# Third sequence's projections ahead of the first feed-forward block, two inputs sent through memory, one weight kept for three products, and ScalarE's pieces placed behind single products

## The chip, the cores and the metric

The kernel runs on one core of one Trainium2 chip. The metric is device time in microseconds. The kernel before took 823.38 us, the median of three runs (822.4 to 823.66).

## What is computed

The input x has 4 sequences of 512 tokens by 512 features, in float32. Each sequence goes through a gated scan and then through a feed-forward block (FFN) with a Walsh-Hadamard transform (fwht) of its 2048 hidden features. Cut to what matters, with `norm` for a layer norm without weights:

```python
def attn(h):                                  # h = norm(x)
    i, f, g = h @ Wi.T, h @ Wf.T, h @ Wg.T    # 512 x 512 each
    gate = sigmoid(f)
    v = silu(i) * (1 - gate)
    o = scan over t of  o[t] = gate[t] * o[t-1] + v[t]
    o = o * rsqrt(mean(o * o) + 1e-5) * gnorm_w * g * sigmoid(g)
    return o @ Wo.T

def ffn(h):                                   # h = norm(x)
    hidden = silu(h @ W1.T) * (h @ W3.T)      # 512 -> 2048
    return fwht(hidden) @ W2.T                # 2048 -> 512

x = x + norm(attn(norm(x)))
x = x + norm(ffn(norm(x)))
```

## The kernel before

**Products.** Every 512x512x512 product is done as seven half-size products of quarter blocks instead of eight (a Strassen-Winograd scheme). `combine_left` and `combine_right` make the sums of blocks S1 to S4 and T1 to T4 with four VectorE operations each. `seven` lists the seven products P1, P2, P6, P5, P7, P3, P4 in this order. Each is eight 128x256 matmuls into one of three PSUM banks X, Y, Z: X serves P1, P6, P7 and P4, Z serves P5 and P3, Y serves P2. P6 adds onto what P1 left in X, so it may start only when ScalarE's copy behind P1 (L418) has read the bank; P3 likewise waits for the copy behind P5, and P4 for VectorE's add behind P7 (L416).

**Units.** A sequence's attention has three units of seven products: (b,0) and (b,1) make i and f for half the features each, (b,2) makes g. At the end of (b,0) and (b,1) `gates` runs on ScalarE and VectorE, ending in the scan; at the end of (b,2) `output_gate` makes `og`, and squares o for the mean square. The out-projection `attn_out(b)` has seven products and one step `squares`, a sum over partitions by 1-column matmuls; its end, `done`, adds the residual (`OutputNorm.half`, whose ScalarE part is L316) and normalizes the result as input 'f' of the FFN (`normalize_tiles`; the scale is applied by ScalarE at L266, after `nb` from VectorE, L233). An FFN has eight units `ffn_unit(b, m)` of seven products and four groups `ffn_out(b, part)` of seven.

**Order.** TensorE's and SP's orders are those of the program text; the other engines' orders are made by a scheduler from priorities (`tc.high_priority`) and from `behind(what)`, which keeps an instruction from going ahead of the latest one of that name on its engine. `run` issues a unit's seven products. After a product it runs what `beside` holds for that place, and, in all places of a dense unit or in places 1, 3, 5 and 6 of another, takes one step from the queue `fill`. In this way out-projections and second FFN products are laid between the products of a unit. Before the change the order is: attention of sequences 0 and 1, FFN 0, attention 2, FFN 1, attention 3, FFN 2, FFN 3; `attn_out(1)` lies in FFN 0, `attn_out(2)` in FFN 1, `attn_out(3)` in FFN 2.

**Transposed inputs.** A normalized input must be turned before it multiplies. For those in `ON_TENSOR` TensorE does it in two steps of eight 128x128 transposes (L348), with copies from PSUM by VectorE and ScalarE (L355, L353). The others go through memory: ScalarE writes the tile in a permuted order, POOL's queue stores it (L275, `xnd`), SP's queue loads it as a `fold` (L371), and VectorE transposes it in 32x32 blocks (L383).

**Weights and buffers.** Weights come through SP's queue in tiles of 896 KB, five buffers in `stream` and four in `stream2`. The first time, a weight is loaded raw (L164), combined, and stored with its sums by POOL's queue (L145); later it is loaded whole (L152). `wo` is loaded for each out-projection by `again`. The matrix W2 is transformed on the way: `transform_high` on TensorE (L646), `butterfly_a` and `butterfly_b` on VectorE with stores by POOL (L665), then `load_low`, `low_pair` and `low_tile` during FFN 0. The pieces of W2 (`w2p`) lie in the buffers `ht` (four) and `stream2`.

Of the kernel before, what the change touches and what calls it, by code (L numbers as in the profile page):

```python
# [14 lines left out]
P = 128  # L15
# [29 lines left out]
def kernel(  # L45
# [56 lines left out]
    beside = {}  # L102

    def run(products, dense):
        for k, make in enumerate(products):
            make()
            for other in beside.pop(k, ()):
                other()
            if dense or k in (1, 3, 5, 6):
                slot()  # L110
# [127 lines left out]
    ON_TENSOR = ("a", 0), ("a", 1), ("f", 0)  # L238
# [124 lines left out]
    def load_fold(b, name):  # L363


        folds[name, b] = t = work.tile(
            [P, T // 32, P], F32, tag="wide", name=f"fold_{name}_{b}", bufs=3
        )
        rows = xnd[name, b].rearrange("t p d -> (t p) d")
        for i in range(4):  # L370
            nc.sync.dma_start(  # L371
                out=t[ts(i, 32)],
                in_=rows[:, ts(i, P)].rearrange("(g q) k -> q g k", q=32),
            )

    def transpose_fold(b, name):


        fold = folds.pop((name, b)).rearrange("p (h g) k -> p h g k", h=2)
        xt = work.tile([P, 7, 2, H], F32, tag="xt", name=f"xt_{name}_{b}", bufs=2)  # L380
        for c in range(ND):
            to = xt[:, B11 : B12 + 1 : B12 - B11] if c < 2 else xt[:, B21 : B22 + 1]
            nc.vector.transpose(  # L383
                to[:, :, c % 2, :].rearrange("p h (g q) -> p h g q", q=32),
                fold[:, :, :, ts(c, 32)],
            )
# [68 lines left out]
    def attn_unit(b, u, dense=False):  # L455
# [14 lines left out]
        def output_gate(d):  # L470
# [7 lines left out]
            nc.scalar.activation(o, o, AF.Square)  # L478
            nc.vector.tensor_add(o[:, 0], o[:, 0], o[:, 1])
            nc.vector.tensor_add(o[:, 0, 0], o[:, 0, 0], o[:, 0, 1])  # L480
# [19 lines left out]
    def attn_out(b):  # L500
# [8 lines left out]
        w = wo_t.pop(b) if b in wo_t else [again(("wo", c), b, stream2) for c in range(2)]  # L509
# [13 lines left out]
        def done(i, j):  # L523
            with tc.high_priority(offset=SOON):
# [3 lines left out]
                if j == 1 - i:  # L528
                    y[1].half(i)
                    normalize_tiles(b, "f", 2 * i, 2)  # L530
# [243 lines left out]
    attn_unit(0, 2)  # L774
    load_attn_w(1, 1)
    fill.extend([None] * 3 + attn_out(0))
    attn_unit(1, 0, True)
    with behind("P7"):
        butterfly_b(2)
        butterfly_a(3)  # L780
        butterfly_b(3)
    load_attn_w(1, 2)
    attn_unit(1, 1, True)
    load_ffn_w(0, 0)
    load_low(0)
    fill.extend([None] + transposes(0, "f"))
    attn_unit(1, 2)
# [3 lines left out]
    LOW = {1: (0, "combined", 0), 3: (1, "P2", 2), 5: (2, "P2", 2), 6: (3, "P2", 2)}  # L791
    for b in range(B):
        last = b == B - 1
        for m in range(NU):
# [13 lines left out]
            if m == 0 and not last:  # L808
                fill.extend([None] * (4 if b else 2) + attn_out(b + 1))
# [6 lines left out]
            if m == 2 and b == 0:  # L816
                load_x(2)
            if m == 4 and b + 2 < B:
                with behind("P7"):
                    late = [normalize_tiles(b + 2, "a", i, 2, True) for i in (0, 2)]  # L820
            if m in (4, 5) and b + 2 < B:
                for t, k in enumerate((3, 5) if m == 4 else (0, 3)):
                    beside.setdefault(k, []).append(
                        partial(behind_copy, partial(late[m - 4], range(t, t + 1)))
                    )
            if m == 6 and not last:
                load_fold(*((b + 2, "a") if b + 2 < B else (b + 1, "f")))
            if m == NU - 1 and not last:
                transpose_fold(*((b + 2, "a") if b + 2 < B else (b + 1, "f")))
# [4 lines left out]
        if b + 2 < B:  # L834
            load_attn_w(b + 2, 0)
            load_fold(b + 1, "f")
            fill.extend([None] + tail)
            for u in range(3):
                if u < 2:
                    load_attn_w(b + 2, u + 1)  # L840
# [47 lines left out]
```

## Time and profile before

| | us |
|---|---|
| median of three runs | 823.38 |
| the profiled execution | 822.66 |
| its span, first to last instruction | 820.9 |
| TensorE matmuls busy | 801.8 (98%) |
| VectorE busy | 492.3 (60%) |
| ScalarE busy | 262.3 (32%) |
| GpSimd busy | 66.3 (8%) |

The span is the time between the first and the last instruction; the profiled execution's own time is 1.8 us more. A busy share says how long an engine had something in work; as matmul records overlap and their ends are modelled, the starts of the records say more about TensorE. The profile's timeline gives instructions in order of time, with an idle time ahead of one and what ended it in brackets. The view of waits adds up such idle times by engine and cause. In names like `X_a<-xt_a,wi` the output stands ahead of the arrow, with the buffer numbers left out; `_a` is attention, `_f` the FFN, `_y` an out-projection and `_po` the second FFN product.

### The profile page before, as it was taken

To read this page: it belongs to the slowest core of one execution; us is meant where nothing else is said; L and a number is where in the kernel's file an instruction comes from. 1 tells how busy PE (TensorE), PEld (TensorE's weight loads), DVE (VectorE), ACT (ScalarE), POOL (GpSimd) and SP (SyncE) were. 2 spreads that over 40 slices of the span, in tenths; PEclk is the share of its full clock that TensorE was granted. 3 is DMA by queue.
4 is the path that set the end of the run, shared out by engine and by line. 5 is a ranking of instruction groups with operands and counts; after the bars stand their busy time and mean duration, and the time that the engine had idled before them with its cause. 6 is when DMAs were issued, how large, how long until landed. Compare 5 with 4: busy or idle time off the path is not lost.

```text
span 820.9 us, 9770 instructions
## 1 busy us (share of the span) xinstructions
PE 801.8 (98%) x3696; PEld 695.9 (85%) x3696; DVE 492.3 (60%) x982; ACT 262.3 (32%) x372; POOL 66.3 (8%) x103
## 2 busy tenths in 40 slices
PE   6999999999999999999999999999999999999995
PEld 4788887888888888888888888888888888888884
DVE  5899789697797457355345646536345334534345
ACT  4553453253321334235312233326211111322111
POOL 2120100122110001011000000102000000100000
PEclk9999999999999999999999999999999999999998
DMA  9985468778998217744538433726463542625201
GB/s 328 406 310 199 142 174 291 260 265 305 332 265 334 91 46 285 310 152 170 229 97 242 161 143 123 288 90 214 156 216 117 208 179 91 235 111 199 80 11 52
DMA packets 64207, 162.19 MB, mean 198 GB/s; under 512 B 4384, under 2 KB 37792, under 8 KB 64160
## 3 DMA queue, kind: packets, MB, share of 16 engines
q1 hardware_dynamic: 55248, 118.31, 41.8%
q0 software_dynamic: 8192, 41.95, 12.9%
q10 hardware_dynamic: 720, 1.31, 0.4%
q8 instruction: 29, 0.48, 0.2%
q14 instruction: 18, 0.15, 0.0%
HBM read 118.56 MB, written 42.99 MB: 197 GB/s over the span
## 4 chain that ended last, share of the span: by engine, by line
PE 88%; DVE 5%; DMA 4%; ACT 1%; issue 1%; SPq 1%; POOL 0%; POOLq 0%; DVEq 0%
PE X_f L431 25%; PE X_po L564 13%; PE Z_f L431 12%; PE X_a L431 8%; PE Z_po L564 7%; PE Y_f L431 6%; PE Z_a L431 4%; PE Y_po L564 3%; PE X_y L517 3%; DMA wo<-s_wo 3%; PE Y_a L431 2%; PE h L646 2%; PE Z_y L517 2%; PE Y_y L517 1%; DVE x L321 1%
## 5 line engine op out<-in xcount | busy, mean ns | idle before, releaser
L431 PE MATMUL X_f<-xt_f,w 128*128 128x256 f32 x1024 | 241.9, 379 | 0.3 <-ACT d_f L418 0.3
L431 PEld LDWEIGHTS X_f<-xt_f,w 128*128 128x128 f32 x1024 | 194.0, 190 | 27.1 <-ACT d_f L418 0.7
L418 ACT COPY d_f<-X_f 128x512 f32<-128x512 f32 x96 | 56.0, 584 | 290.9 <-PE X_f L431 266.6
L431 PE MATMUL Z_f<-xt_f,w 128*128 128x256 f32 x512 | 121.1, 379 | 1.1 <-ACT d_f L418 1.1
L564 PE MATMUL X_po<-w,ht 128*128 128x256 f32 x512 | 120.9, 379 | 0.2 <-DVE f L416 0.2
L431 PEld LDWEIGHTS Z_f<-xt_f,w 128*128 128x128 f32 x512 | 97.2, 190 | 14.7 <-ACT d_f L418 1.5
L564 PEld LDWEIGHTS X_po<-w,ht 128*128 128x128 f32 x512 | 97.2, 190 | 13.7 <-DVE f L416 0.6
L416 DVE TENSOR_TENSOR f<-X_po,f 128x512 f32<-128x512 f32 x51 | 35.1, 687 | 93.8 <-PE X_po L564 87.6
L446 DVE TENSOR_TENSOR ht<-d_f 128x1024 f32<-128x1024 f32 x32 | 39.0, 1219 | 62.6 <-ACT d_f L540 48.9
L564 PE MATMUL Z_po<-w,ht 128*128 128x256 f32 x256 | 60.5, 379 | 0.0
L431 PE MATMUL Y_f<-xt_f,w 128*128 128x256 f32 x256 | 60.5, 379 | 0.0
L564 PEld LDWEIGHTS Z_po<-w,ht 128*128 128x128 f32 x256 | 48.6, 190 | 6.6
L431 PEld LDWEIGHTS Y_f<-xt_f,w 128*128 128x128 f32 x256 | 48.6, 190 | 6.6
L418 ACT COPY d_a<-X_a 128x512 f32<-128x512 f32 x36 | 21.0, 583 | 89.9 <-PE X_a L431 81.7
L225 POOL TENSOR_TENSOR rs_f<-rs_f,power 128x2 f32<-128x2 f32 x16 | 14.2, 891 | 416.4 <-DVE nm_f L313 395.9
L416 DVE TENSOR_TENSOR d_f<-X_f,d_f 128x512 f32<-128x512 f32 x32 | 22.1, 690 | 27.7 <-PE X_f L431 27.7
L416 DVE TENSOR_TENSOR d_f<-Z_f,d_f 128x512 f32<-128x512 f32 x32 | 22.1, 690 | 22.1 <-PE Z_f L431 22.1
L540 ACT ACTIVATE d_f<-d_f 128x1024 f32<-128x1024 f32 x32 | 33.8, 1055 | 0.9
L431 PE MATMUL X_a<-xt_a,wi 128*128 128x256 f32 x128 | 33.2, 382 | 0.8 <-ACT w2p L647 0.7
L431 PE MATMUL X_a<-xt_a,wf 128*128 128x256 f32 x128 | 32.8, 379 | 0.0
L517 PE MATMUL X_y<-wo,og 128*128 128x256 f32 x128 | 30.7, 380 | 0.9 <-DMA wo<-s_wo 0.8
L416 DVE TENSOR_TENSOR f<-Z_po,f 128x512 f32<-128x512 f32 x28 | 19.2, 686 | 20.5 <-PE Z_po L564 20.5
(163 smaller groups left out, 1007.3 us busy)
## 6 DMA issues: line engine op xcount, KB each, us to landing
w<-s_w SPq DMA_DIRECT2D x72, 896.0 KB, 6.4
s_w<-w POOLq DMA_DIRECT2D x24, 896.0 KB, 6.9
w<-in_W_dram SPq DMA_DIRECT2D x32, 256.0 KB, 5.6
wi<-s_wi SPq DMA_DIRECT2D x6, 896.0 KB, 10.6
wf<-s_wf SPq DMA_DIRECT2D x6, 896.0 KB, 6.7
wg<-s_wg SPq DMA_DIRECT2D x6, 896.0 KB, 5.8
wo<-s_wo SPq DMA_DIRECT2D x6, 896.0 KB, 9.3
w_h<-w2p POOLq DMA_DIRECT2D x8, 512.0 KB, 5.9
```

Of the source, the lines that this page charges most:

```text
L225: read["power"] = nc.gpsimd.tensor_tensor(r, r, power_t[:, 0:n], ALU.pow)
L321: nc.vector.scalar_tensor_tensor(x_t, self.y[:, i, t, :], r[:, t : t + 1], x_t, ALU.mult, ALU.add)
L416: read[what] = nc.vector.tensor_add(to, ps[which], to)
L418: read["copy"] = nc.scalar.copy(to, ps[which])
L431: nc.tensor.matmul(ps[:, n, :], w[:, a, c, :], xt[:, bb, c, :], start=first and n == 0 and c == 0, stop=c == 1, skip_group_check=True,)
L446: nc.vector.tensor_mul(to.rearrange("p (t k) f -> p k t f", t=2), a.rearrange("p k (t f) -> p k t f", t=2), b2.rearrange("p k (t f) -> p k ...
L517: nc.tensor.matmul(ps[:, t, :], og[:, a, c, ts(t, P)], w[c][:, bb, :], start=first and t == 0 and c == 0, stop=c == 1, skip_group_check=True,)
L540: nc.scalar.activation(d[:, 0], d[:, 0], AF.Silu)
L564: nc.tensor.matmul(ps[:, t, :], hts[b, m][:, a, ts(t, P)], w[m][:, W2[bb], :], start=first and t == 0 and m == ms[0], stop=m == ms[-1], sk ...
L646: nc.tensor.matmul(p, h_sb, t[:, k, :], start=True, stop=True)
```

## The change

It makes six edits.

1. `acts` is a new queue of ScalarE pieces. `run` takes one of them after each product and places it behind the latest copy. The scaling of input 'f' (four pieces per sequence) and the Square of `output_gate`, now in two halves, go there.
2. The first FFN's input leaves `ON_TENSOR` and goes through memory.
3. The three attention units of sequence 2 stand ahead of FFN 0, with `attn_out(1)` between their products; `attn_out(2)` lies in FFN 0, and `attn_out(3)` in FFN 2 as before. The normalized input of sequence 2 is made beside unit (1,1), stored, loaded as a fold after it, and transposed beside unit (1,2). The fold of FFN 0's input is loaded after unit (2,0) and transposed beside the last products of (2,1).
4. A fold is now two tiles of 128 KB DMAs, eight loads instead of four, and eight VectorE transposes of 128x256 instead of four of 128x512; a fold may lie in two `ht` buffers.
5. The weight `wo` that is loaded for sequence 0 stays in its two buffers for sequences 1 and 2; only sequence 3 loads it again.
6. The butterflies `butterfly_b(2)`, `butterfly_a(3)` and `butterfly_b(3)` move from behind unit (1,0) to unit (2,0); x of sequences 2 and 3 is loaded at other places.

```diff
@@ -100,10 +100,14 @@
                 make()
 
     beside = {}
+    acts = deque()
 
     def run(products, dense):
         for k, make in enumerate(products):
             make()
+            if acts:
+                with behind("copy"):
+                    acts.popleft()()
             for other in beside.pop(k, ()):
                 other()
             if dense or k in (1, 3, 5, 6):
@@ -235,7 +239,7 @@
 
     xns, xnd = {}, {}
 
-    ON_TENSOR = ("a", 0), ("a", 1), ("f", 0)
+    ON_TENSOR = ("a", 0), ("a", 1)
 
     def normalize_tiles(b, name, i0, n, later=False):
 
@@ -360,30 +364,39 @@
 
     folds = {}
 
-    def load_fold(b, name):
-        folds[name, b] = t = work.tile(
-            [P, T // 32, P], F32, tag="wide", name=f"fold_{name}_{b}", bufs=3
-        )
+    def load_fold(b, name, tag="wide"):
+        G = T // 64
+        if tag == "ht":
+            t = [
+                work.tile([P, G, P], F32, tag=tag, name=f"fold_{name}_{b}_{h}", bufs=4)
+                for h in range(2)
+            ]
+        else:
+            both = work.tile([P, 2, G, P], F32, tag=tag, name=f"fold_{name}_{b}", bufs=3)
+            t = [both[:, h] for h in range(2)]
+        folds[name, b] = t
         rows = xnd[name, b].rearrange("t p d -> (t p) d")
-        for i in range(4):
-            nc.sync.dma_start(
-                out=t[ts(i, 32)],
-                in_=rows[:, ts(i, P)].rearrange("(g q) k -> q g k", q=32),
-            )
+        for h in range(2):
+            for i in range(4):
+                nc.sync.dma_start(
+                    out=t[h][ts(i, 32)],
+                    in_=rows[ts(h, H), ts(i, P)].rearrange("(g q) k -> q g k", q=32),
+                )
 
     def transpose_fold(b, name):
 
 
-        fold = folds.pop((name, b)).rearrange("p (h g) k -> p h g k", h=2)
+        fold = folds.pop((name, b))
         xt = work.tile([P, 7, 2, H], F32, tag="xt", name=f"xt_{name}_{b}", bufs=2)
-        for c in range(ND):
-            to = xt[:, B11 : B12 + 1 : B12 - B11] if c < 2 else xt[:, B21 : B22 + 1]
-            nc.vector.transpose(
-                to[:, :, c % 2, :].rearrange("p h (g q) -> p h g q", q=32),
-                fold[:, :, :, ts(c, 32)],
-            )
+        for h in range(2):
+            for c in range(ND):
+                to = xt[:, (B11, B12)[h] if c < 2 else (B21, B22)[h], c % 2]
+                nc.vector.transpose(
+                    to.rearrange("p (g q) -> p g q", q=32), fold[h][:, :, ts(c, 32)]
+                )
         combine_right(xt, nc.vector)
         xts[name, b] = xt
 
@@ -475,9 +488,14 @@
                 into_left(og, o[:, m], d[:, m], m)
             combine_left(og, nc.vector)
             ogs[b] = og
-            nc.scalar.activation(o, o, AF.Square)
-            nc.vector.tensor_add(o[:, 0], o[:, 0], o[:, 1])
-            nc.vector.tensor_add(o[:, 0, 0], o[:, 0, 0], o[:, 0, 1])
+            def square(m):
+                nc.scalar.activation(o[:, m], o[:, m], AF.Square)
+                if m:
+                    nc.vector.tensor_add(o[:, 0], o[:, 0], o[:, 1])
+                    nc.vector.tensor_add(o[:, 0, 0], o[:, 0, 0], o[:, 0, 1])
+            acts.extend(partial(square, m) for m in range(2))
 
         project(
             attn_w.pop((b, u)), xts["a", b], f"a_{b}_{u}", gates if u < 2 else output_gate,
@@ -506,7 +524,7 @@
 
 
         y = {}
-        w = wo_t.pop(b) if b in wo_t else [again(("wo", c), b, stream2) for c in range(2)]
+        w = wo_t[0] if b < 3 else [again(("wo", c), b, stream2) for c in range(2)]
 
         def multiply(ps, a, bb, first):
             og = ogs[b]
@@ -527,7 +545,8 @@
                 y[1].quarter(i, j)
                 if j == 1 - i:
                     y[1].half(i)
-                    normalize_tiles(b, "f", 2 * i, 2)
+                    apply = normalize_tiles(b, "f", 2 * i, 2, True)
+                    acts.extend(partial(apply, range(t, t + 1)) for t in range(2))
 
         steps = seven(f"y_{b}", multiply, lambda i, j: y[0][:, i, :, ts(j, H)], done)
         return steps[:4] + [partial(squares, b)] + steps[4:]
@@ -772,25 +791,54 @@
 
     fill.extend([wo_behind_sum, partial(behind_copy, *apply)] + transposes(1, "a"))
     attn_unit(0, 2)
+    load_x(2)
     load_attn_w(1, 1)
+    def beside_copies(b, places):
+        with behind("P7"):
+            late = [normalize_tiles(b, "a", i, 2, True) for i in (0, 2)]
+        for t, place in enumerate(places):
+            yield place, partial(behind_copy, partial(late[t // 2], range(t % 2, t % 2 + 1)))
+    def transpose_beside(b, name, k=1, what="P2"):
+        def step():
+            with behind(what):
+                transpose_fold(b, name)
+        beside.setdefault(k, []).append(step)
     fill.extend([None] * 3 + attn_out(0))
     attn_unit(1, 0, True)
-    with behind("P7"):
-        butterfly_b(2)
-        butterfly_a(3)
-        butterfly_b(3)
     load_attn_w(1, 2)
+    for k, step in beside_copies(2, range(NT)):
+        beside.setdefault(k, []).append(step)
     attn_unit(1, 1, True)
+    load_fold(2, "a", "ht")
+    load_attn_w(2, 0)
+    transpose_beside(2, "a")
+    attn_unit(1, 2)
+    load_attn_w(2, 1)
+    fill.extend([None] * 3 + attn_out(1))
+    for k, make, g in ((1, butterfly_b, 2), (2, butterfly_a, 3), (3, butterfly_b, 3)):
+        low_step(k, "P2", make, g)
+    attn_unit(2, 0, True)
+    load_attn_w(2, 2)
+    load_fold(0, "f", "ht")
+    transpose_beside(0, "f", 6, "P3")
+    attn_unit(2, 1, True)
     load_ffn_w(0, 0)
     load_low(0)
-    fill.extend([None] + transposes(0, "f"))
-    attn_unit(1, 2)
+    attn_unit(2, 2)
     with behind("P7"), tc.high_priority(offset=SOON):
         combine_weights()
 
     LOW = {1: (0, "combined", 0), 3: (1, "P2", 2), 5: (2, "P2", 2), 6: (3, "P2", 2)}
+    NEXT = (1, "f"), (3, "a"), (3, "f")
     for b in range(B):
         last = b == B - 1
+        late = {}
         for m in range(NU):
             if b == 0 and m == 3:
                 load_low(1)
@@ -805,54 +853,47 @@
                 low_step(k, what, low_pair, p)
                 for t in range(NS):
                     low_step(k + 1 + t, what, low_tile, NS * p + t)
-            if m == 0 and not last:
-                fill.extend([None] * (4 if b else 2) + attn_out(b + 1))
+            if m == 0 and b in (0, 2):
+                fill.extend([None] * (4 if b else 2) + attn_out(2 if b == 0 else 3))
             if m and m % NS == 0:
                 if last and m == NU - NS:
                     fill.extend([None] * 8)
                 fill.extend([None] + ffn_out(b, m // NS - 1))
             if b and m % NS == 1:
                 load_down_w(b, m // NS)
-            if m == 2 and b == 0:
-                load_x(2)
-            if m == 4 and b + 2 < B:
-                with behind("P7"):
-                    late = [normalize_tiles(b + 2, "a", i, 2, True) for i in (0, 2)]
-            if m in (4, 5) and b + 2 < B:
-                for t, k in enumerate((3, 5) if m == 4 else (0, 3)):
-                    beside.setdefault(k, []).append(
-                        partial(behind_copy, partial(late[m - 4], range(t, t + 1)))
-                    )
+            if b == 1 and m == 3:
+                load_x(3)
+            if b == 1 and m == 4:
+                late = dict(beside_copies(3, ((4, 3), (4, 5), (5, 0), (5, 3))))
+            for (unit, k), step in late.items():
+                if unit == m:
+                    beside.setdefault(k, []).append(step)
             if m == 6 and not last:
-                load_fold(*((b + 2, "a") if b + 2 < B else (b + 1, "f")))
+                load_fold(*NEXT[b])
             if m == NU - 1 and not last:
-                transpose_fold(*((b + 2, "a") if b + 2 < B else (b + 1, "f")))
+                transpose_fold(*NEXT[b])
             ffn_unit(b, m)
             with behind("P7"), tc.high_priority(offset=SOON):
                 combine_weights()
         tail = ffn_out(b, NU // NS - 1)
-        if b + 2 < B:
-            load_attn_w(b + 2, 0)
-            load_fold(b + 1, "f")
+        if b == 1:
+            load_attn_w(3, 0)
             fill.extend([None] + tail)
             for u in range(3):
                 if u < 2:
-                    load_attn_w(b + 2, u + 1)
+                    load_attn_w(3, u + 1)
                 else:
-                    load_ffn_w(b + 1, 0)
+                    load_ffn_w(2, 0)
+                    transpose_beside(2, "f")
                 if u == 1:
-                    transpose_fold(b + 1, "f")
-                attn_unit(b + 2, u)
-            if b + 3 < B:
-                load_x(b + 3)
+                    load_fold(2, "f", "ht")
+                attn_unit(3, u)
         elif not last:
             load_ffn_w(b + 1, 0)
             fill.extend([None] + tail)
         else:
             fill.extend(tail)
             flush()
```

## The prediction

> **What bounds the kernel now.** I read the page's first table, then the waits of TensorE, then TensorE's timeline beside ScalarE's where a wait shows.
>
> ```profile
> PE 801.8 (98%) x3696; PEld 695.9 (85%) x3696; DVE 492.3 (60%) x982; ACT 262.3 (32%) x372; POOL 66.3 (8%) x103
> ```
>
> TensorE is the bound, but its 98% hides little: steady groups of eight 128x256 products start 1.73 us apart, 0.216 us a product, and no edit here makes one shorter. So the change can take only two things from TensorE: operations that are not products, and idle gaps. The waits view lists the gaps' causes, its columns being total us, times and longest.
>
> ```profile
> PE Z_f L431 <- ACT d_f L418: 1.1, 1, 1.1
> PE X_y L517 <- DMA wo<-s_wo: 0.8, 1, 0.8
> PE X_a L431 <- ACT d_a L418: 0.6, 1, 0.6
> PE X_f L431 <- ACT d_f L418: 0.3, 1, 0.3
> ```
>
> All are single events. TensorE's timeline places them; the reader is to see the two transposes between products and the bracketed idle times.
>
> ```profile
> 105.33 1.99 PE L431 MATMUL X_a<-xt_a,wg 128*128 128x256 f32 x8 [0.62 <-ACT d_a L418]
> 107.17 1.89 PE L431 MATMUL Z_a<-xt_a,wg 128*128 128x256 f32 x8
> 108.89 1.11 PE L348 MATMUL pt_f<-ident,xn_f 128*128 128x128 f32 x8
> 109.84 1.89 PE L431 MATMUL X_a<-xt_a,wg 128*128 128x256 f32 x8
> ...
> 125.86 1.99 PE L431 MATMUL Z_f<-xt_f,w 128*128 128x256 f32 x8 [1.09 <-ACT d_f L418]
> ...
> 129.08 1.53 PE L517 MATMUL X_y<-wo,og 128*128 128x256 f32 x6 [0.79 <-DMA wo<-s_wo]
> ```
>
> The end of a matmul record is not when the next can start, so I measure gaps between starts: what a step has over the usual 0.216 us, with the 0.07 to 0.10 us by which the step after a gap is long too. That gives 0.89 us at 105, 1.36 at 125, 1.03 at 129, 0.41 at 328.4 (out-projection of sequence 2, at wo again) and 0.54 at 514 (ScalarE). ScalarE's timeline says why at 105 and 125:
>
> ```profile
> 100.51 1.52 ACT L266 ACTIVATE xn_f<-x,nb_f,rs_f 128x512 f32<-128x512 f32 x2 [3.81 <-DVE nb_f L233]
> 101.93 1.32 ACT L316 ACTIVATE y<-y,nm_y 128x512 f32<-128x512 f32 x2
> 103.16 0.56 ACT L418 COPY d_a<-X_a 128x512 f32<-128x512 f32 x1
> 103.75 1.06 ACT L459 ACTIVATE d_a<-d_a 128x1024 f32<-128x1024 f32 x1
> 104.71 0.57 ACT L418 COPY d_a<-X_a 128x512 f32<-128x512 f32 x1
> ```
>
> P6 accumulates into the bank that the copy behind P1 still reads; that copy stood behind 3.9 us of other ScalarE work. At 125 it is the Square (L478, 1.91 us at 123.43), which waited for VectorE's og and held up the P5 copy until 125.24.
>
> [...] a ready copy waited behind a piece that was not. [...] the records say 282 ns, but eight of them move the next product by only 0.95 us, which is the price I use. [...]
>
> **The change, part by part.**
>
> (1) *Transposes of the first FFN's input off TensorE.* Two groups of eight go: 2 x 0.95 = **−1.90 us**. In their place: a write, eight fold loads and VectorE transposes. VectorE loses 6 copies of 0.41 us, ScalarE 2 of 0.38; VectorE gains 8 transposes 128x256. That shape is not in the trace: at least half of L383's 684 ns, at most all of it; I take 0.42 us, as of 128x256 copies, so 3.4 us against 2.5. The five other folds go from 4 x 0.68 to 8 x 0.42, +0.6 us each. All of this lies on VectorE (60% busy); ends: 0 if products cover it, 1.5 us if it delays an add that P4 waits for. ScalarE's pieces for this norm go from 0.8 to 1.35 us each (xn_a's shortest and longest), as they now write the permuted form.
>
> (2) *wo kept.* Four loads of 896 KB go, with both wo waits: 1.03 + 0.41 = **−1.44 us**. The buffers stay taken until sequence 2's out-projection is done in the first FFN's first three units; low pair 0 takes the other two, so nobody waits for them before pair 2. The fourth product loads wo as before, under four empty slots, and did not wait.
>
> (3) *ScalarE pieces behind products.* The Square becomes two of about 1.05 us (L459 has that size), and the norm pieces of 'f' lose their raised priority and go one per product. That removes 0.89 + 1.36 + 0.54 = **−2.79 us**, if each piece fits between two copies (a copy has 1.1 us to spare when no other product lies between). A half Square that waits for og still blocks: I leave **+0.3 us**. In units (1,1) to (1,2) eight permuted pieces meet the gates: **+0.3 us**. Ends: 0 and 1.5 us together.
>
> (4) *The moved order.* Units, slots and leftover slots are equal in number, so product time is unchanged. The three butterfly calls (12 instructions of 0.69 us, 8.3 us of VectorE, and 4 POOL stores) leave units (1,0) and (1,1) for (2,0), which has the shape (1,0) had; statistics of sequence 2 (four of 0.68 us) take their place. The load of x for sequence 2 moves to about 48 us, in a slice where the DMA engines are 0.8 busy, past wi of (1,1) alone: four issues, 2 us, for a weight that landed at 59 and is wanted at 83: 0. POOL gets two stores of normalized tiles more (12 instead of 10, 0.75 us each), beside TensorE: 0, since the powers that it computes take 0.7 us each with idle time ahead of them.
>
> The place that can hurt is the passage from (1,2) to (2,0). From the before's timeline (1,1) starts at 82.93 and ends at 101.1. The last norm piece of sequence 2 stands behind the P5 copy (94.4 to 95.0) and two others: done by 97.9. Its store lands 3.7 us after issue (xnd_a), so at about 101.7. SP then issues four fold loads, 2 us by the fold rows; the DMAs land 6 to 8 us after issue where others run, so 108 to 110. **Queued behind them on SP** are wi and wf of (2,0), 0.33 us each to issue. A row of 896 KB loads elsewhere lands 2.1 us apart, so they land near 110.3 and 112.4. (2,0) starts at 101.1 + 7 x 1.73 = 113.2, and wf is first used 0.9 us later. Margin about 1.7 us for wf and 3 for wi. VectorE meanwhile may sit on a transpose whose fold has not landed, with P7's add behind it, for which P4 waits at 111.5. T2 for P6 is wanted only at 116.7. I take **0**; ends −0 and +5.
>
> The second fold (sequence 0's 'f') waits for the butterfly stores, about 135, lands by 146 to 153 and is wanted from 150 for a unit that starts at 162: covered by 12 us of (2,2). Without that cover it would cost up to 3 us. From the second FFN on all is as before, only later: x of sequence 3 must be in before its statistics, 12 us into that unit, and lands about 10 us into it; 0, at worst 2.
>
> Sum: −1.90 − 1.44 − 2.79 + 0.6 = −5.5 us. The profiled execution is 822.66 us (span 820.9 and 1.8 around it), so 817.1; the median of the runs shown, 823.38, is 0.7 higher: **817.9 us**.
>
> **Rivals.**
>
> *A: the fold comes a little late.* The xnd store or its fold slips by 2 to 6 us, as fold_f did (13.5 us to landing against 7.1 for fold_a). [...] Against: this stretch loses the raw weight loads and their stores. It costs 1 to 4 us at P1 of (2,0) or P4 of (1,2): 819 to 822.
>
> *B: slower, through one order on ScalarE.* If the last norm piece of sequence 2 is placed behind sequence 0's 'f' pieces, it waits for nb_f of the second half, ready at 106.7 before. Then four pieces of 1.35 us and it: 112 to 113; store landed 117; wi and wf 8.6 and 10.7 us after that, at 126 to 128 against 113.2. Stall 13 us, less 5.5: about 831. If only the first two 'f' pieces (nb_f at 100.4) stand ahead of it: done 104.5, landed 109, stall 5 to 6, hence 823 to 824. Each microsecond of the store past about 103.4 costs one; past about 109 the change is slower. For it: ScalarE has nearly 20 us of work for the 18 us of (1,1): gates 3.3, copies and centrings 6.1, eight pieces 10.6. Against: the 'a' pieces have all they need by 86, the 'f' pieces not before 100.
>
> *C: the gaps only move.* TensorE's ScalarE waits reappear behind the permuted pieces, and only the transposes and wo count: −3.3, 820. If VectorE also loses 1.5 us: 821.6, hardly told from no change.
>
> **How the numbers follow.** A measurement of this kernel can tell about 0.2%, 1.65 us, from no change, so "faster" is below 821.7. The forecast has 0.42; A 0.22, of it 0.03 within; B 0.20, of it 0.03 within; C 0.16, of it 0.03 within. So faster 0.74, same 0.09, slower 0.17. The range goes from 816.4 (all gaps gone, with some of the 0.9 us that stand between 60 and 67) to 824.0, through A, C and B's mild end; B's far end is left out.
>
> **What would show it.** Right: 32 transposes L348 on TensorE instead of 48; L478 eight times near 1.05 us; 2 wo loads; no wait of TensorE for wo or for L418 above 0.5 us; first product of the first FFN about 46 us later (28 products of 1.73 us, squares 0.8, less 1.9 and 0.9). Wrong: a wait of TensorE for wi, wf or xt_a near 112 to 117, or of VectorE for fold_a near 105; SP standing at a fold load past 104. If the (1,2) to (2,0) passage has a gap over 5 us, the forecast is wrong.

## The result, and the profile after

The changed kernel takes 824.61 us, the median of 20 runs (824.05 to 826.62); the kernel before, measured beside it, takes 823.16 (822.02 to 824.0). The ratio is 1.002, with a 95% interval from 1.0013 to 1.0026: it is slower by 1.45 us, where 5.5 us less had been forecast. That is less than the 1.65 us that the prediction would have called no change, but the interval excludes a ratio of 1. The profiled span is 823.0 us against 820.9.

The first table of the page after, with busy time, share of the span and count, answers to the first line shown of before:

```profile
PE 801.1 (97%) x3680; PEld 694.0 (84%) x3680; DVE 492.5 (60%) x1004; ACT 264.2 (32%) x374; POOL 66.5 (8%) x105
```

Sixteen operations left TensorE, as they should, and its busy time fell by only 0.7 us while the span grew by 2.1. So the loss is idle time. The waits of TensorE after (us in total, times, longest):

```profile
PE X_a L444 <- ACT d_a L431: 4.2, 3, 1.7
...
PE X_a L444 <- DVE d_a L429: 1.4, 3, 0.9
```

The wait for wo and the two on `X_f` and `Z_f` that the view showed before are gone. In their place stand waits of attention's own products, L444, for ScalarE's copy (L431) and VectorE's add (L429). TensorE's timeline places them:

```profile
106.87 1.99 PE L444 MATMUL X_a<-xt_a,wg 128*128 128x256 f32 x8 [1.66 <-ACT d_a L431]
...
111.47 1.99 PE L444 MATMUL X_a<-xt_a,wg 128*128 128x256 f32 x8 [0.88 <-ACT d_a L431]
...
115.48 1.78 PE L444 MATMUL X_a<-xt_a,wg 128*128 128x256 f32 x7 [0.28 <-DVE d_a L429]
...
159.73 1.99 PE L444 MATMUL X_a<-xt_a,wg 128*128 128x256 f32 x8 [1.65 <-ACT d_a L431]
...
168.09 1.99 PE L444 MATMUL X_a<-xt_a,wg 128*128 128x256 f32 x8 [0.94 <-DVE d_a L429]
```

All of these lie in two units of the same kind: (1,2), where `attn_out(0)` has just ended, and (2,2), where `attn_out(1)` has. (The third wait for VectorE, 0.18 us at 507.86, lies in (3,2).) Each is the g unit of a sequence, whose start meets the gates of the unit ahead. P6 is late at 106.87 and 159.73, P7 at 111.47, P4 at 115.48 and 168.09. The prediction's sign of being right, no wait for ScalarE's copy above 0.5 us, is broken three times.

**The balance.** By the measure of the prediction (what a step of TensorE has over the usual step of its operation), summed over all steps from the same place of the program on, at about 63 us, the kernel before loses 4.47 us and the changed one 7.88: +3.41. Less the 1.90 us of transposes that makes +1.51, and the medians differ by +1.45, so no other loss is left to explain. The stretch ahead of 63 us is left out because it differs between executions of one kernel: P6 of (1,2) starts at 106.87 here and at 105.98 in experiment 11, the same kernel again. Place by place:

| | before | after |
|---|---|---|
| (1,2): P6 / P7 / P4 | 0.89 / 0 / 0 | 1.92 / 1.15 / 0.55 |
| first unit of FFN 0 in before: Square, then wo | 1.36 / 1.03 | 0 / 0 |
| (2,2): P6 / P3 / P4 | 0 | 1.91 / 0.23 / 1.21 |
| wo of sequence 2 | 0.41 | 0 |
| (3,2): P4; and the first FFN unit after it | 0 / 0.54 | 0.45 / 0.17 |

ScalarE's timeline after shows what stands ahead of the copies:

```profile
101.04 2.52 ACT L270 ACTIVATE xn_f<-x,nb_f,rs_f 128x512 f32<-128x512 f32 x2 [2.64 <-DVE nb_f L237]
103.46 1.32 ACT L320 ACTIVATE y<-y,nm_y 128x512 f32<-128x512 f32 x2
104.69 0.57 ACT L431 COPY d_a<-X_a 128x512 f32<-128x512 f32 x1
105.29 1.06 ACT L472 ACTIVATE d_a<-d_a 128x1024 f32<-128x1024 f32 x1
106.25 0.57 ACT L431 COPY d_a<-X_a 128x512 f32<-128x512 f32 x1
...
108.40 2.54 ACT L270 ACTIVATE xn_f<-x,nb_f,rs_f 128x512 f32<-128x512 f32 x2 [0.63 <-DVE nb_f L237]
110.85 0.57 ACT L431 COPY d_a<-X_a 128x512 f32<-128x512 f32 x1
```

The chain is the one that the prediction showed of before, in the same order: two pieces L270, two pieces L320 of the output norm (the centrings), the P4 copy of the unit ahead, a piece of the gates, and then at 106.25 the copy that P6 waits for. Only the first item has grown, from 1.52 to 2.52 us, because the pieces of sequence 0 are now permuted. Both pieces of a half still run back to back: ScalarE stood idle for 2.64 us until `nb_f` came, and then had both. The second pair, at 108.40, does the same to the P6 copy at 110.85, for which P7 waits.

VectorE's timeline shows the late P4 of (1,2) and of (2,2):

```profile
112.50 2.34 DVE L479 TENSOR_TENSOR_SCAN o<-d_a 128x512 f32<-128x512 f32 x2 [1.01 <-ACT d_a L475]
114.76 0.67 DVE L429 TENSOR_TENSOR d_a<-X_a,d_a 128x512 f32<-128x512 f32 x1
...
163.35 0.65 DVE L140 TENSOR_TENSOR xt_f<-xt_f 128x512 f32<-128x512 f32 x1
163.92 2.33 DVE L479 TENSOR_TENSOR_SCAN o<-d_a 128x512 f32<-128x512 f32 x2
166.16 0.67 DVE L141 TENSOR_TENSOR xt_f<-xt_f 128x512 f32<-128x512 f32 x1
166.75 0.68 DVE L142 TENSOR_TENSOR xt_f<-xt_f 128x512 f32<-128x512 f32 x1
167.35 0.68 DVE L429 TENSOR_TENSOR d_a<-X_a,d_a 128x512 f32<-128x512 f32 x1
```

In (1,2) P7's add, L429, stands behind two scans, and these had waited 1.01 us for a gate of ScalarE (L475), which stood behind the second pair of pieces. In (2,2) it comes behind both scans and two sums T (L141, L142) of FFN 0's input, which no product needs before the first one of the FFN, at 169.9.

**The DMA**, where the forecast put its risk, did no harm. The last store of `xnd` for sequence 2 landed at 101.31, the fold at 103.7 to 106.4, and wi and wf of (2,0) at 109.5 and 112.6. TensorE never waited for them.

### The profile page after: what moved, and what is told of

Read it like the earlier page. It is cut to its first block, busy times and chain, and to the rows that moved or that the text cites. A ratio compares the mean times of both kernels' runs of the same rounds, so it can differ in the third digit from the quotient of the medians.

```text
span 823.0 us, 9805 instructions
## 1 busy us (share of the span) xinstructions
PE 801.1 (97%) x3680; PEld 694.0 (84%) x3680; DVE 492.5 (60%) x1004; ACT 264.2 (32%) x374; POOL 66.5 (8%) x105
## 4 chain that ended last, share of the span: by engine, by line
PE 89%; DVE 6%; ACT 2%; issue 1%; DMA 1%; POOL 0%; POOLq 0%; DVEq 0%; SPq 0%
PE X_f L444 27%; PE Z_f L444 13%; PE X_po L583 13%; PE X_a L444 7%; PE Y_f L444 7%; PE Z_po L583 7%; PE Y_po L583 3%; PE Z_a L444 3%; PE X_y L535 3%; PE Y_a L444 2%; PE h L665 2%; PE Z_y L535 2%; PE Y_y L535 1%; ACT xn_f L270 1%; DVE o L479 1%
## 5 line engine op out<-in xcount | busy, mean ns | idle before, releaser
L444 PE MATMUL X_f<-xt_f,w 128*128 128x256 f32 x1024 | 242.0, 379 | 0.0
L444 PEld LDWEIGHTS X_f<-xt_f,w 128*128 128x128 f32 x1024 | 194.2, 190 | 26.7 <-ACT d_f L431 0.3
L431 ACT COPY d_f<-X_f 128x512 f32<-128x512 f32 x96 | 56.1, 585 | 320.9 <-PE X_f L444 304.7
L444 PE MATMUL Z_f<-xt_f,w 128*128 128x256 f32 x512 | 121.0, 379 | 0.0
L444 PEld LDWEIGHTS Z_f<-xt_f,w 128*128 128x128 f32 x512 | 97.3, 190 | 13.2
L429 DVE TENSOR_TENSOR f<-X_po,f 128x512 f32<-128x512 f32 x51 | 35.0, 687 | 85.4 <-PE X_po L583 85.4
L444 PE MATMUL Y_f<-xt_f,w 128*128 128x256 f32 x256 | 60.5, 379 | 0.0
L444 PEld LDWEIGHTS Y_f<-xt_f,w 128*128 128x128 f32 x256 | 48.6, 190 | 6.6
L429 DVE TENSOR_TENSOR d_f<-X_f,d_f 128x512 f32<-128x512 f32 x32 | 22.0, 689 | 43.7 <-PE X_f L444 40.7
L431 ACT COPY d_a<-X_a 128x512 f32<-128x512 f32 x36 | 20.9, 582 | 57.4 <-PE X_a L444 57.3
L444 PE MATMUL X_a<-xt_a,wg 128*128 128x256 f32 x128 | 31.0, 385 | 5.7 <-ACT d_a L431 4.2
L429 DVE TENSOR_TENSOR d_f<-Z_f,d_f 128x512 f32<-128x512 f32 x32 | 22.0, 689 | 22.4 <-PE Z_f L444 22.4
L444 PE MATMUL X_a<-xt_a,wi 128*128 128x256 f32 x128 | 33.1, 381 | 0.8 <-ACT w2p L666 0.7
L444 PEld LDWEIGHTS X_a<-xt_a,wg 128*128 128x128 f32 x128 | 23.7, 190 | 11.6 <-ACT d_a L431 5.4
L444 PE MATMUL X_a<-xt_a,wf 128*128 128x256 f32 x128 | 32.9, 379 | 0.0
```

The source lines that it names most:

```text
L429: read[what] = nc.vector.tensor_add(to, ps[which], to)
L431: read["copy"] = nc.scalar.copy(to, ps[which])
L444: nc.tensor.matmul(ps[:, n, :], w[:, a, c, :], xt[:, bb, c, :], start=first and n == 0 and c == 0, stop=c == 1, skip_group_check=True,)
```

## The experiments

Two theories are tried. The theory S: the changed order puts pieces and sums, in two places, ahead of copies and adds for which TensorE waits, and the size of what stands there is the loss. The main rival V: VectorE's added work sets the time, and ScalarE's copies are late only as its shadow. Each kernel was run beside the kernel before, on the same chip, and the differences are taken to that.

**1. The pieces of the first half held back.** Six empty places in `acts` ahead of the 'f' pieces of a first half, so that they come behind the g unit's copies.

```diff
             if acts:
-                with behind("copy"):
-                    acts.popleft()()
+                piece = acts.popleft()
+                if piece is not None:
+                    with behind("copy"):
+                        piece()
...
+                    acts.extend([None] * (6 if i == 0 else 0))
                     acts.extend(partial(apply, range(t, t + 1)) for t in range(2))
```

> The changed kernel with one more edit: six empty places are put ahead of the four scaling pieces of an 'f' input, so that they are issued behind products P6 to P3 of the next unit, when their scales have long been ready. Theory S (the two pieces of a half wait for their scales, and then run back to back, 2.5 us, ahead of copies that TensorE waits for): the waits of TensorE near 105, 110, 158 and 167 us go, each now 1 to 1.9 us, and the 0.4 us near 115; 824.6 falls by 5 to 6.5 us, to 818 to 819.5. Theory V (VectorE is too late in units (1,2) and (2,2), by the transposes and the scans): its work and order are nearly the same, the waits only change their name; at most 2 us go, 822.5 or more.

820.28 us against 822.62, ratio 0.9973 (0.9963 to 0.9984). ScalarE's timeline of this kernel, in the same passage:

```profile
100.40 1.33 ACT L322 ACTIVATE y<-y,nm_y 128x512 f32<-128x512 f32 x2 [3.52 <-DVE nm_y L319]
...
103.20 0.57 ACT L433 COPY d_a<-X_a 128x512 f32<-128x512 f32 x1
...
108.11 1.31 ACT L272 ACTIVATE xn_f<-x,nb_f,rs_f 128x512 f32<-128x512 f32 x1
109.32 0.56 ACT L433 COPY d_a<-Z_a 128x512 f32<-128x512 f32 x1
```

The centrings now come first, and the P1 copy stands at 103.20. P6's gap falls from 1.92 to 0.40 in (1,2) and from 1.91 to 0.36 in (2,2), and P7's is gone. One piece is in front of the P5 copy at 109.32, so P3 now waits 0.94 us. The edit touches ScalarE's pieces alone, and some 3.6 us came back, as S says. VectorE's order shifted with them in places, though: in (2,2) two of the four sums stand ahead of P7's add, and no longer three. So this run alone does not part S from V; 2 and 10 do. It stops 0.8 us above S's upper figure, for this new wait and for VectorE's three, of which 0.76 at P4 of (2,2) is the largest.

**2. The same pieces, plain.** FFN inputs written in plain order, hence shorter pieces. The step that would set their features right again is left out, so this kernel computes something else; its times alone are used.

```diff
-                if (name, b) not in ON_TENSOR:
+                if (name, b) not in ON_TENSOR and name != "f":
```

> The changed kernel, with the scaling pieces of 'f' writing in plain instead of permuted order (the features of the FFN inputs then stand in another order, which is left uncorrected). Only the length of the pieces changes, 1.27 to about 0.77 us; ScalarE's order in units (1,1) and (1,2) is that of the changed kernel. Theory S: each pair takes 1.5 instead of 2.5 us, so each of the four large waits shrinks by about 1.0 us (1.8 to 0.8, 1.05 to 0.1): 3 to 4 us in all, 820.5 to 821.5. Theory V: less than 1 us.

821.02 us against 822.62, ratio 0.9982 (0.9975 to 0.9989).

```profile
101.14 1.52 ACT L270 ACTIVATE xn_f<-x,nb_f,rs_f 128x512 f32<-128x512 f32 x2 [2.62 <-DVE nb_f L237]
```

The pair is 1.52 us again, 1.00 less than with the permuted form. P6's gap in (1,2) is 0.92, 1.00 less; in (2,2) it is 0.89, 1.02 less; P7's fell from 1.15 to 0.12. The order of operations on ScalarE and on VectorE is that of the changed kernel throughout, so the length of a pair passes into P6's wait one for one, and V has no part in this gain. P4 of (2,2) went from 1.21 to 1.53, since everything ahead of it on TensorE comes earlier and VectorE's sums do not.

**3. FFN 0's input on TensorE again**, in the new order; its fold and VectorE transposes go.

```diff
-    ON_TENSOR = ("a", 0), ("a", 1)
+    ON_TENSOR = ("a", 0), ("a", 1), ("f", 0)
...
-    load_fold(0, "f", "ht")
-    transpose_beside(0, "f", 6, "P3")
...
+    fill.extend([None] + transposes(0, "f"))
     attn_unit(2, 2)
```

> The changed kernel, with the first FFN's input turned on TensorE again (two groups of eight transposes in unit (2,2), no store, no fold): edit 2 is undone, the moved order stays. Theory S: TensorE gets 1.9 us of transposes back; the pieces of sequence 0 become plain, so the waits near 105 and 110 fall by about 1 us each; sequence 1's pieces stay permuted and the wait near 158 stays at 1.8 us. In all 824 to 825. Theory V: VectorE loses 6.1 us of transposes and sums in (2,1) and (2,2) and gets 5.2 back: no more than the transposes, 826.5.

823.89 us against 822.62, ratio 1.0014 (1.0008 to 1.0021). With 1.90 us of transposes back on TensorE the time is that of the changed kernel within 0.2 us, measured from before; S expected 824 to 825, V 826.5. In (1,2) P6's gap is 0.92 and P7's 0.09; in (2,2) P6 keeps its 1.90, which comes from sequence 1's pieces, still permuted; P4's 1.21 is gone, but gaps of 0.20 and 0.27 stand behind the two steps of transposes, and 0.30 and 0.78 at the first FFN products, the larger for ScalarE's copy. So edit 2 gains next to nothing in this order: what TensorE saves in transposes it loses again behind longer pieces and later adds.

**4. Edit 5 (for two sequences) and the Square in halves alone, on the kernel before.**

```diff
+            if acts:
+                with behind("copy"):
+                    acts.popleft()()
...
-            nc.scalar.activation(o, o, AF.Square)
...
+            acts.extend(partial(square, m) for m in range(2))
...
-        w = wo_t.pop(b) if b in wo_t else [again(("wo", c), b, stream2) for c in range(2)]
+        w = wo_t[0] if b < 2 else [again(("wo", c), b, stream2) for c in range(2)]
```

> The kernel before with two parts of the change alone: wo kept for sequences 0 and 1, and the Square in two halves behind products. Both theories: the waits at 125 (1.36 us), 129 (1.03) and 514 (0.54) go, the waits at 105 (0.89) and at 328 (0.41, third wo) stay: 823.2 falls by 2.5 to 2.9 us, to 820.3 to 820.7. If it falls by less than 1.5 us, those gaps were not worth their length.

821.07 us against 822.62, ratio 0.9981 (0.9973 to 0.9989): a gain of 1.55 us, about 1 us short of what was expected. The wait for wo of sequence 1 (1.03) is gone; the Square's went from 1.36 to 0.50, not to 0, as a half that waits for `og` still stands ahead of a copy; and the wait for wo of sequence 2, which this kernel still loads, grew:

```profile
327.67 1.56 PE L526 MATMUL X_y<-wo,og 128*128 128x256 f32 x6 [0.97 <-DMA wo<-s_wo]
```

By starts that is 1.24 us instead of 0.41. A wait for a DMA is the difference of two times: TensorE came to this product 2.1 us earlier than in before (326.10 against 328.18), and the second tile landed only 1.3 us earlier (327.62 against 328.88). The two edits work in the old order too, at less than the sum of the waits that they remove.

**5. The norm pieces issued at once**, without the queue `acts`.

```diff
-                    apply = normalize_tiles(b, "f", 2 * i, 2, True)
-                    acts.extend(partial(apply, range(t, t + 1)) for t in range(2))
+                    normalize_tiles(b, "f", 2 * i, 2)
```

> The changed kernel, with the scaling pieces of 'f' issued at once and with raised priority, as in the kernel before; the Square stays in halves behind products. Theory S says that a piece ends up where its scale becomes ready, wherever it was queued: ScalarE's sequence comes out the same as in the changed kernel, so 824.6 within 0.5 us, and the waits near 105 and 110 stay at 1.8 and 1.0 us. If placing the pieces behind single products had helped, it is slower by 1 us or more.

823.78 us against 822.5, ratio 1.0018 (1.0011 to 1.0024); every gap of TensorE is the same as after, P6 1.92, P7 1.15, P4 0.55, and so on, and so is the order of operations on every engine. For the 'f' pieces edit 1 does nothing: the product behind which they are placed is long past when `nb_f` comes.

**6 and 7. Delay, and VectorE's folds moved.** In 6, seven empty places, the last two pieces with a place between, and the second half of the fold of (2,a) transposed behind P7 of (1,2). In 7, the fold of FFN 2's input loaded and transposed a unit earlier as well.

```diff
+                    pieces = [partial(apply, range(t, t + 1)) for t in range(2)]
+                    if i == 0:
+                        acts.extend([None] * 7 + pieces)
+                    else:
+                        acts.extend([pieces[0], None, pieces[1]])
...
-    transpose_beside(2, "a")
+    transpose_beside(2, "a", halves=(0,))
+    transpose_beside(2, "a", 4, "P7", halves=(1,))
```

> The run with delayed pieces, with seven empty places instead of six, a free place ahead of the fourth piece, and the second half of the fold of sequence 2 transposed behind P7's add of (1,2) instead of ahead of it. What is left there is VectorE: P7's add came 0.4 us late behind transposes at 112 us, and ScalarE's Identity of the gates stood behind a piece at 158, which made the scans and P7's add 0.7 us late; P5's copy came 0.8 us late at 109. With all three gone 820.3 falls by 1.5 to 2 us, to 818.3 to 818.8. If VectorE is simply full there, less than 0.7 us.

> The same, and the fold of sequence 2's 'f' loaded one unit earlier and transposed beside (3,1) instead of (3,2). The wait near 502 to 507 (0.35 + 0.10 us, P4 of (3,2) for P7's add) is put down to the transposes that stand there together with the statistics of the first output norm: without them it goes, 0.4 us less than the run with delayed pieces and split fold. If it is the statistics alone, no difference.

819.2 and 819.44 us against 822.5; both ratios 0.9962 (0.9949 to 0.9974, and 0.995 to 0.9975). Measured from before, 6 gains 1.0 us on experiment 1, where 1.5 to 2 were expected. P3's wait in (1,2) is gone in both, but P4's in (2,2) grew to 1.53: the adds moved closer to TensorE's need, and the sums stood where they were. In 7 the 0.45 us of (3,2) is gone too, but the 0.4 us that this should bring does not show in the times of 6 and 7.

**8. wo loaded for each sequence again**, everything else as changed.

```diff
-        w = wo_t[0] if b < 3 else [again(("wo", c), b, stream2) for c in range(2)]
+        w = wo_t.pop(b) if b in wo_t else [again(("wo", c), b, stream2) for c in range(2)]
```

> The changed kernel, with wo loaded again for sequences 1 and 2, as before (edit 5 undone). If keeping wo is worth what the prediction said, the waits of the first out-projection product come back: 1.0 us in (2,0) or in the first FFN and 0.4 us or more, 825.5 to 826. If the moved order hides these loads, as there is no raw weight load ahead of them in (2,0), only that in the first FFN comes back, or none: 824.6 to 825.2.

831.71 us against 822.5, ratio 1.0112 (1.0097 to 1.0127): 8 us over the changed kernel, far more than either figure. TensorE's timeline of this kernel:

```profile
125.84 1.53 PE L535 MATMUL X_y<-wo,og 128*128 128x256 f32 x6 [1.47 <-DMA wo<-s_wo]
...
185.84 1.54 PE L535 MATMUL X_y<-wo,og 128*128 128x256 f32 x6 [3.64 <-DMA wo<-s_wo]
187.22 3.58 PE L444 MATMUL X_f<-xt_f,w 128*128 128x256 f32 x8
```

The two tiles for sequence 2 were issued at 171.8 and 172.5 and landed at 181.4 and 185.7, 9.6 and 13.3 us later. By starts the two waits cost 1.70 and 3.88 us, an og that is late 0.49, and the slow product behind the long wait 1.65 (the last section has more on it): 7.7 of the 8. The kernel before also loads wo in FFN 0, for sequence 1, at a cost of 1.03: its second tile landed 11.7 us after issue and was wanted after 10.8. Here the second tile landed after 13.3 us and was wanted after 9.6; why it took 1.6 us longer these runs do not show. Without keeping wo the new order would have cost 9.2 us instead of 1.3.

**9. VectorE's sums held back too**: 7, and the four sums of FFN 0's input moved behind P7's add of (2,2).

```diff
-    transpose_beside(0, "f", 6, "P3")
+    transpose_beside(0, "f", 6, "P3", sums=False)
...
+    def sums_behind_add():
+        with behind("P7"):
+            combine_right(xts["f", 0], nc.vector)
+
+    beside.setdefault(4, []).append(sums_behind_add)
     attn_unit(2, 2)
```

> The run with delayed pieces, split fold and early fold of sequence 2's 'f', and besides the four sums of the first FFN's input (L142 to L145 there) behind P7's add of (2,2). In that run P7's add came 1.4 us late, as two of these sums and two scans stood ahead of it; without the sums that wait should go to 0.3 us or less: about 818 against the 822.5 of before, a ratio of 0.9945. If the scans alone hold the add, half of it, 818.7.

**817.8 us** against 822.47, ratio 0.9946 (0.9934 to 0.9959): faster than both kernels, and the best version found. TensorE's timeline in (1,2):

```profile
104.14 1.99 PE L450 MATMUL X_a<-xt_a,wg 128*128 128x256 f32 x8
105.97 1.89 PE L450 MATMUL Z_a<-xt_a,wg 128*128 128x256 f32 x8
107.69 1.89 PE L450 MATMUL X_a<-xt_a,wg 128*128 128x256 f32 x8
109.42 1.89 PE L450 MATMUL Z_a<-xt_a,wg 128*128 128x256 f32 x8
111.53 1.99 PE L450 MATMUL X_a<-xt_a,wg 128*128 128x256 f32 x8 [0.22 <-DVE d_a L435]
```

P6, P7 and P3 have no idle time in brackets any more, and P4 has 0.22 us. By starts P6 keeps 0.39 and P4 0.49 here, and in (2,2) the 1.53 us at P4 are 0.32. The sums were the larger part of that wait, and the time is the one expected.

**10 and 11. VectorE's order alone, and the changed kernel again beside 9.** 10 is the changed kernel with the fold of (2,a) in halves and the sums late, and ScalarE's pieces as they were.

> The changed kernel with only VectorE's order mended: the second half of sequence 2's fold transposed behind P7's add of (1,2), and the four sums of the first FFN's input behind P7's add of (2,2); ScalarE's pieces stay where they are. Theory S: the three ScalarE waits (1.8, 1.05 and 1.8 us) stay; only the waits for P7's add (0.45 and 1.1 us) can go, and partly, as the scans wait for ScalarE: 823 to 824. Theory V: with VectorE in time most goes: 820 or less.

> The changed kernel itself, on the same chip as the two others. All theories: 1.5 us above the kernel before, a ratio of 1.001 to 1.003.

10 takes 822.42 us against 822.47, ratio 1.0006 (0.9998 to 1.0014); the changed kernel on that chip 823.77, ratio 1.0018 (1.0011 to 1.0025).

```profile
PE X_a L448 <- ACT d_a L435: 4.2, 3, 1.7
...
PE X_a L448 <- DVE d_a L433: 0.5, 2, 0.3
```

ScalarE's 4.2 us stay to the tenth, and of VectorE's 1.4 us the 0.9 at P4 of (2,2) is gone. S expected 823 to 824 with before at 823.2; before took 0.7 us less on this chip, so S holds. The copies are late whatever VectorE does, so V is refuted as the main cause. Its part, taken alone, is 1.3 us, all of it at the sums: P4 of (1,2) still loses 0.55 us, although four of the fold's transposes stand ahead of the add instead of six: the scans ahead of it wait for ScalarE, now for 1.66 us. The four kernels nearly make a square; relative to before each changes, in us:

| | VectorE as changed | VectorE mended |
|---|---|---|
| ScalarE as changed | +1.3 (11) | 0 (10) |
| ScalarE mended | −2.3 (1) | −4.7 (9) |

Mending ScalarE alone gives 3.6 us, VectorE alone 1.3, both 6.0. The square is not a clean one: 9 has from 6 and 7 also one more empty place, a spacing and an earlier fold. From 1 to 9 the gaps fall by 0.94 (P3 of (1,2)), 0.23 (P3 of (2,2)), 0.44 (P4 of (2,2)) and 0.63 (in and behind (3,2)), 2.2 us in all where the times fall by 2.3. So the 1.1 us over the sum of the two parts cannot be put to VectorE's order alone.

The balance of starts holds for the experiments as well, to 0.6 us, with one profiled execution of each set against a median. The sum of gaps from 63 us on, less that of before, less 1.90 where the transposes are gone, against the difference of the medians:

| | gaps | by the balance | measured |
|---|---|---|---|
| 1 | 4.10 | −2.27 | −2.34 |
| 2 | 4.91 | −1.46 | −1.60 |
| 3 | 5.89 | +1.42 | +1.27 |
| 4 | 3.28 | −1.19 | −1.55 |
| 6 | 3.65 | −2.72 | −3.30 |
| 7 | 3.05 | −3.32 | −3.06 |
| 8 | 16.07 | +9.70 | +9.21 |
| 9 | 1.80 | −4.57 | −4.67 |
| 10 | 6.63 | +0.26 | −0.05 |

## Why the prediction was wrong

Two terms failed by the same mechanism: pieces that start together when their operand comes (2.52 us of them at 101.04, 2.54 at 108.40), ahead of a copy for which TensorE waits. Step (3) counted 0.89 us at P6 of (1,2) as removed, and that unit lost 2.73 us more instead. Step (4) put the moved order at 0, and (2,2) lost 3.35 us, 1.91 of it in this way.

**Step (1), transposes: right on TensorE, wrong in what it put at nothing.** 32 transposes are left on TensorE instead of 48, and the balance closes with the trace's own price, 0.95 us per eight. The prediction's entry for VectorE was right as a sum (the 128x256 transposes are recorded at 0.41 us, 0.42 was assumed), but "all of this lies on VectorE" left out where on VectorE. It kept 1.5 us as an end "if it delays an add that P4 waits for", and P4 of (2,2) does lose 1.21: the sums behind the transposes stand ahead of the add, and moving the sums takes this away (experiment 10). The 0.55 at P4 of (1,2) is not of this kind, as experiment 10 leaves it as it is. In before eight transposes on TensorE (113.30 to 114.25) stood ahead of that P4, and the add ended under them, at 113.52. Its note that the pieces "go from 0.8 to 1.35" was made and not carried to the wait that it had shown at 105: a piece measures 1.27, and the pair stood in the very chain that the prediction had quoted. Experiment 2 shows that the pair's 1.00 us passes one for one into P6's wait, and into P7's: 2.03 of the 2.73 us that (1,2) lost.

**Step (2), wo: right, and too small for this order.** Two tiles of wo are loaded and no wait for them is left. The step counted the waits that it saw in before, 1.44 us. In the new order the edit is worth 8 us (experiment 8), which never showed in the sum because the price was of the old places.

**Step (3), pieces behind products: the step that failed.** "The norm pieces of 'f' go one per product. That removes 0.89 + 1.36 + 0.54." The Square's 1.36 did go (eight halves of 1.06 us, and no wait for them); at 514, 0.37 of 0.54 went. But `behind` only keeps a piece from going ahead of a copy. The piece also has to have its operand, and VectorE's last step for `nb_f` starts at 100.85 and 108.21. I had both numbers for before, 100.4 and 106.7, and used them in rival B for another purpose. So the 0.89 us that was to vanish became 1.92, 1.15 came beside it, and experiment 5 shows that the queue changed nothing for these pieces. With the first pair held back by six places (experiment 1), P6 keeps 0.40 and P7 nothing, and one piece costs P3 0.94. What failed was an inference of mine, that a place in the program is a place in time. In the trace a piece that waits holds up the copy behind it: P6's record in (1,2) ends at 108.86, and its copy starts at 110.85, behind a pair of 2.54 us that had waited for `nb_f` until 108.40.

**Step (4), the moved order: right on DMA, wrong on what moves with it.** The xnd store was forecast at 101.7 and landed at 101.31, wi and wf at 110.3 and 112.4 and landed at 109.5 and 112.6; the fold came earlier than stated. The first FFN product comes 54 us later (115.98 to 169.9), not 46; the gaps of (1,2) and (2,2) make up 7.0 us of this. The "0" was wrong for a thing that the step did not list: the end of `attn_out(1)`, its residual, norm and four pieces, moved from FFN 0, where no gates are, into (2,1) and (2,2), where it meets gates, copies and scans just as `attn_out(0)` does in (1,2). That is one more chain of the kind shown at 105, and it cost 1.91 at P6, and 1.44 at P3 and P4, 1.21 of it behind the sums of FFN 0's input. "Queued behind" was worked out for SP's queue and not for ScalarE's.

**The sum.** Against before, (1,2) came out 2.73 us worse, where (3) had it 0.89 better; (2,2) 3.35 worse, where (4) had 0; (3,2) 0.45 worse. Gone are 1.90 + 1.36 + 1.03 + 0.41 + 0.37 = 5.07. That leaves +1.5. The forecast of −5.5 is missed by 7.0: 0.89 that step (3) did not remove, 2.03 from longer pieces in (1,2), 0.70 more there (0.55 of it at P4), 3.35 in (2,2), and 0.63 in and behind (3,2), less the 0.6 that had been put aside.

**The rivals.** A, the fold late, did not occur; B's order did not either, the 'a' piece came in time. C, "the gaps only move", named the right mechanism, "waits reappear behind the permuted pieces", but let them come back at their old size, 820, at most 821.6. They came back at twice the size and in one place more, so C had to reach above before's time and did not. None of the signs of being wrong that the prediction named came up: all looked at the fold and the weights of (2,0), and the loss came from ScalarE and VectorE.

## What to carry to other kernels

When work is put behind a named instruction, ask when its operands arrive: here they came later, the two pieces of a half ran together when they came (2.52 us, after 2.64 us of idle time), and the copies behind them waited, which left TensorE a gap of 1.92 us at P6. When a stage is moved, list what its end issues on each engine and lay it over what the new neighbours need there; count the length of each piece into the waits already in the profile, one for one (experiment 2: 1.00 us off a pair took 1.00 and 1.02 us off the gaps at P6). And after one engine's order is mended, look at the next engine's before judging the change: here the same six edits are worth +1.3 us, or −4.7 us with another order on ScalarE and VectorE.

## What the runs showed of the hardware

Experiment 8 holds one surprise. After the idle time of 3.64 us TensorE went on near its usual step for 1.4 us, and then one product took 3.37 us from its start to the next (187.22 to 190.59), 0.42 us a step where 0.216 is usual; the product behind it took 1.76. The view by windows (us, busy time and instructions of the five engines, granted clock, DMA share, GB/s) has it in the clock, 1.00 in the windows on both sides and 0.66 in the one between; half the clock for 3.37 of its 5 us would make 0.66, an estimate from these numbers:

```profile
180.00:186.00 6.00, 2.36 (x12) 1.66 (x11) 5.97 (x15) 0.00 (x0) 1.07 (x2) 1.00 1.04 406
186.00:191.00 5.00, 5.00 (x16) 4.07 (x16) 1.41 (x4) 0.76 (x2) 0.00 (x0) 0.66 0.79 315
191.00:196.00 5.00, 5.00 (x25) 4.41 (x24) 3.39 (x7) 2.06 (x3) 0.00 (x0) 1.00 0.65 192
```

So 1.65 us came on top of this one idle time. Shorter waits show no such fall: behind the 1.47 us at 125.84 in the same run, four steps are recorded at 1.03 us as elsewhere, and in the changed kernel, with up to 1.66 us of idle time in (1,2) and (2,2), the clock is 1.00 in every window of 5 us from 100 to 135 and from 155 to 170. What brings the clock down and what brings it back, these runs do not show.

The other thing not expected is how much a permuted access costs ScalarE: 1.27 us for a piece of 128x512 that reads its input in steps of four elements against 0.76 in plain order (half of a pair: 2.54 us in the changed kernel, 1.52 in experiment 2), the same operation otherwise.
